# Four bias additions of a two-layer graph kernel: from GpSimd arithmetic to accumulating DMAs

## The chip, the cores and the metric

The kernel runs on one core of one Trainium2 chip. The metric is the device time of one execution in microseconds. A core has five engines with a queue of instructions each, executed in the order of the queue: TensorE (PE; its weight loads are listed as PEld), VectorE (DVE), ScalarE (ACT), GpSimd (POOL) and SyncE (SP). SP and GpSimd also issue DMAs; 16 DMA engines move the data.

## The reference, cut to what matters

There are 32 batches of 512 nodes with 256 features, in float32. Two layers follow one another, each with a graph part and a feed-forward part, and each part adds its result to x:

```python
# layer 0
x = x + gnn(layernorm(x), adj)
h = layernorm(x)
trop = piecewise(max over features of (h + Wt))          # 1024 columns
fused = g * trop + (1 - g) * gelu(h @ Wc + bc)           # g = sigmoid(h @ Wg + bg)
x = x + fused @ Wd + bd                                  # <- bd
# layer 1
h = einsum('bnd,hde->bhne', layernorm(x), W)             # 4 heads of 64
attention = softmax(leaky_relu(e_src + e_dst), masked by adj)
dst = attention @ h + bias                               # <- the bias of the values
out = relu(dst) + h
out = (out - mean) / sqrt(var + eps) * ln_gamma + ln_beta   # <- ln_beta
x = x + out
sw = softmax(layernorm(x) @ Wslice')                     # 512 columns, 64 slices of 8 heads
x = x + (sw @ scan(tokens)) @ out_w.T + out_b            # <- out_b
```

The four marked rows are the biases of this case: `bd` of layer 0's feed-forward, and of layer 1 `gnn_bias` (called abias), `ln_beta` (beta) and `out_b` (outb). As a softmax row sums to one, adding abias to the values before the weighted sum and adding it to the weighted sum afterwards give the same dst.

## The kernel before

The kernel is written in Python that is unrolled in full. A scheduling layer then orders each engine's queue with a cost model of its own and puts in the semaphores, so that the source order and the order on an engine differ; the source still steers it, by generators that are woven into one another.

**Layer 0** (`layer0_sorted`). The nodes are sorted by how many table rows they need. `feed_forwards` goes through 32 groups of 512 nodes. `sums(s, g)` gathers the group's rows into `xg` with four indirect DMAs (L553; a row has 275 numbers: 256 features, mean, count and the like). For each of four tiles of 128 nodes, ACT normalizes into `xn` (L574), GpSimd issues gathers of table rows (L564, L595), and DVE folds every row into `best` by a maximum (L598). At the end of `sums`, L609 to L610 add bd to the four tiles of `xg`, one GpSimd addition of 128 x 256 numbers each. `mixed` runs the two dense matmuls (L623), their activations (L625), and the bends of the piecewise function (L632 to L641). `down` multiplies by Wd (L652), adds the product to `xg` on DVE (L654), and stores the sum (L655). `down` of a group stands one group later than its `sums`. The convolutions of the later nodes are woven in between (L392 to L470).

**Layer 1** (`layer1_plain`). `attentions` handles one batch after another, and `prepare(b + 1)` is woven into `attention(b)`; `mixer` (the second part of the layer, `slices`, `tokens`, `scan`, `unslice`) takes two batches at a time and draws the attentions along with it: each `yield` of `mixer` names a number, which is multiplied by PACE, and so many steps of `attentions` follow.

`prepare(b)` gathers x by four indirect DMAs (L1154), normalizes it (`normed`, L1126 to L1133), and then adds beta to the stored x by one GpSimd addition of 128 x 1024 numbers (L1167). PE computes the heads' values and logits (hp, L1180) for four tiles; of each tile ACT takes three exponentials, `mine` (L1183), the factor in column HO of `hv` (L1184) and `other` (L1185), and copies the values to `ht` (L1186). Then GpSimd writes `ht` plus abias to `hv` (L1189), and DVE multiplies `hv` by the factor, in four instructions (L1202). Meanwhile `mine` goes by a PE transpose (minep, L1193), an ACT copy, a store (L1197) and four broadcasting loads (L1200) into the rows `own`, which the attention steps need.

`attention(b)` has 8 turns. In each, DVE makes two tiles of weights (`weigh`, L1213: the larger of own and other, times the mask), three turns ahead; PE multiplies them with `hv` (avp, L1249) and sums them (adp, L1254). At the end the sums are transposed back (L1232), and DVE divides into `av` (L1275). `norm(b, av)` is drawn step by step during the next batch's turns, through the list `unfinished`: its first step applies the relu and adds `ht` (L1290) and takes means (L1292 to L1294); its second gets the variance, with a power on GpSimd (L1300), and multiplies by gamma (L1301); its third scales (L1303) and adds to x (L1304). It is drawn after turns 0, 1 and 3.

`slices(b)` normalizes x again (L1126 to L1133), adds outb to the stored x with one GpSimd addition (L1328), and makes the slice weights (lgp, L1335 to L1342) and tokens (yTp, L1347). `scan` mixes the tokens (xp L1400 to vp L1557, with y at L1520 to L1522, yTp L1527, oTp L1535, msp L1543, rms L1546 and L1547). `unslice` multiplies back and adds to x (L1567, L1569), which is stored (L1570).

PSUM has two sets of four banks in layer 1: tag "pv" for attention's sums, and tag "any" for all other products (hp, x3T, x4T, lgp, minep, yTp and so on), handed out again when the last reader of a bank is done.

Of the kernel before, what the change touches and what calls it, by code (L numbers as in the profile page):

```python
# [8 lines left out]
F32 = mybir.dt.float32  # L9
# [4 lines left out]
AF = mybir.ActivationFunctionType  # L14
ALU = mybir.AluOpType
# [4 lines left out]
P = 128  # L20
N = 512
D = 256
# [75 lines left out]
def layer0_sorted(tc, ident, eps, x, adj, w, x2s, ranks, over, following):  # L98
# [29 lines left out]
    with ExitStack() as ctx:  # L128
# [4 lines left out]
        def const(name, shape, src):  # L133
            t = cst.tile(shape, F32, tag=name, name=name)
            nc.sync.dma_start(t, src)
            return t
# [3 lines left out]
        bias = const("bias", [P, D], w["bias"].partition_broadcast(P))  # L140
        bd = const("bd", [P, D], w["bd"].partition_broadcast(P))
        wc = cst.tile([P, DC, FFN], F32, tag="wc", name="wc")
# [31 lines left out]
        for c in range(CT // P):  # L174
            nc.gpsimd.affine_select(below[:, c, :], below[:, c, :], pattern=[[1, CT]], compare_op=ALU.is_gt,
                                    fill=0.0, base=-c * P, channel_multiplier=-1)

        table = dr.tile([D, FFN], F32, tag="table", name="table", bufs=1)
        least = dr.tile([2, D], F32, tag="least", name="least", bufs=1)
# [363 lines left out]
        def feed_forwards():  # L543


            def sums(s, g):
# [57 lines left out]
                for c in range(DC):  # L604
# [3 lines left out]
                                        ALU.is_gt)  # L608
                for t in range(NT):  # L609
                    nc.gpsimd.tensor_add(xg[:, t, :D], xg[:, t, :D], bd)  # L610
                got[s, g] = xg, xnT, best
# [253 lines left out]
def layer1_plain(tc, ident, eps, x2s, ranks, adj, w, out, over, ps):  # L865
# [23 lines left out]
    TURNS = AP * NT + 6  # L889
    STEPS = 15  # L890
    WANTED = 68
# [9 lines left out]
    with ExitStack() as ctx:  # L901
# [41 lines left out]
        edges = ctile("edges", [P, 2, B * NT])  # L943
        abias = const("abias", [P, AH * HO], w["gnn_bias"].rearrange("h e -> (h e)").partition_broadcast(P))
        gamma = const("gamma", [P, AH * HO], w["ln_gamma"].rearrange("h e -> (h e)").partition_broadcast(P))
        beta = const("beta", [P, AH * HO], w["ln_beta"].rearrange("h e -> (h e)").partition_broadcast(P))
        bfx = const("bfx", [P, KC, 1], w["b_fx"].rearrange("(k p o) -> p k o", p=P, o=1))
        bfx_eps = ctile("bfx_eps", [P, KC])
        nc.vector.tensor_scalar_mul(bfx_eps, bfx[:, :, 0], -1e-5)
        outb = const("outb", [P, D], w["out_b"].partition_broadcast(P))  # L950
        conv_w = const("conv_w", [P, KC, KW], w["hy_conv_w"][:DI].rearrange("(c p) k -> p c k", p=P))
# [196 lines left out]
        def prepare(b):  # L1148
# [13 lines left out]
            for i, _ in enumerate(edged):  # L1162
                if i < 3 or b not in masked:
                    yield
                if i == 2:
                    normed(xt, xn, f"c{b}")
                    nc.gpsimd.tensor_add(xt, xt, beta.unsqueeze(1).to_broadcast([P, NT, D]))  # L1167
                    yield
# [8 lines left out]
            for t in range(NT):  # L1177
                ph = psum("any", f"hp{b}_{t}")
                for c in range(DC):
                    nc.tensor.matmul(ph[:, : AH * (HO + 2)], xnT[:, c, t * P : (t + 1) * P], wa[:, c, :],  # L1180
                                     start=c == 0, stop=c == DC - 1)
                d = ph[:, AH * HO : AH * HO + AH]
                nc.scalar.activation(mine[:, :, t], ph[:, AH * (HO + 1) : AH * (HO + 2)], AF.Exp, scale=1.0 - SLOPE)  # L1183
                nc.scalar.activation(hv[:, t, :, HO], d, AF.Exp)  # L1184
                nc.scalar.activation(other[:, t, :], d, AF.Exp, scale=SLOPE - 1.0)  # L1185
                nc.scalar.copy(ht[:, t, :], ph[:, : AH * HO])  # L1186
                yield

            nc.gpsimd.tensor_add(hv[:, :, :, :HO], ht.rearrange("p t (h e) -> p t h e", h=AH),  # L1189
                                 abias.rearrange("p (h e) -> p h e", h=AH).unsqueeze(1).to_broadcast([P, NT, AH, HO]))  # L1190
            yield
            pt = psum("any", f"minep{b}")
# [6 lines left out]
            for h in range(AH):  # L1199
                nc.sync.dma_start(own[h], own_row[h].partition_broadcast(P))  # L1200
            for t in range(NT):
                nc.vector.tensor_mul(hv[:, t, :, :HO], hv[:, t, :, :HO], hv[:, t, :, HO:].to_broadcast([P, AH, HO]))  # L1202
            ready[b] = mask, ht, hv, other, own
# [12 lines left out]
        def attention(b):  # L1216
# [21 lines left out]
            for i, (q, j) in enumerate(turns):  # L1238
# [17 lines left out]
                yield  # L1256
                if unfinished and i != 2:
                    next(unfinished[0], None)
                    yield
                    if i > 2:  # L1260
                        unfinished.pop()
# [10 lines left out]
            for q in range(AP):  # L1272
                bt = back(vT[q], f"bp{q}_")
                heads = slice(2 * q, 2 * q + 2)
                nc.vector.tensor_mul(av[:, :, heads, :], bt.rearrange("p (t h e) -> p t h e", t=NT, h=2),  # L1275
                                     rs[:, :, heads].unsqueeze(3).to_broadcast([P, NT, 2, HO]))
                yield
            unfinished.append(norm(b, av))

# [38 lines left out]
        def slices(b, j, yT, rn):  # L1318
# [8 lines left out]
            xnT = yield from turned(xn, "x4T", f"x4T{b}", 1)  # L1327
            nc.gpsimd.tensor_add(xt, xt, outb.unsqueeze(1).to_broadcast([P, NT, D]))  # L1328
            sw = sb.tile([P, NT, DI], F32, tag="sw", name=f"sw{b}", bufs=1)
# [910 lines left out]
```

## Time and profile before

Each of three runs took 4456.45, 4460.33 and 4473.15 us; the median is 4460.33. The profiled execution took 4459.08 us, of which the span from the first instruction to the last is 4456.4.

| engine | busy us | share of the span |
|---|---|---|
| PE | 3922.0 | 88% |
| DVE | 3347.2 | 75% |
| ACT | 2291.6 | 51% |
| POOL | 1718.8 | 39% |

The four additions in GpSimd's table of instructions:

| line | what | count | busy us | mean ns |
|---|---|---|---|---|
| L610 | `xg` + bd, 128 x 256 | 128 | 109.6 | 861 |
| L1189 | `hv` = `ht` + abias, 128 x 1024 | 32 | 80.2 | 2506 |
| L1167 | x + beta, 128 x 1024 | 32 | 77.6 | 2424 |
| L1328 | x + outb, 128 x 1024 | 32 | 75.8 | 2370 |

A line of the timeline has the start, the time that the instructions took together, the engine, the source line, the operation, output and inputs, the shapes, the number of instructions, and in brackets the idle time of the engine before them and what ended it. A line of the list of waits has the waiting instruction, who ended the wait, and the total, the number and the longest of these waits. The chain of waits goes back from the last instruction, at each step to what released it.

### The profile page before, as it was taken

Reading aid. Unit: us, or ns where it says so; the run is one execution under the profiler, and the core shown is the slowest. Engines: PE = TensorE matmul, PEld = TensorE weight load, DVE = VectorE, ACT = ScalarE, POOL = GpSimd, SP = SyncE. Lnnn points to the kernel's source line nnn. Section 1 sums busy time; section 2 is a strip of 40 time slices with the busy share of each in tenths; the row PEclk is TensorE's granted clock in tenths of the full one; section 3 lists DMA queues with packets and bytes.
Section 4 is the critical chain, followed back from the end, with each engine's and each line's share of the span. In section 5 each row is a group of like instructions: output and inputs, shape, how many; then the busy total and the mean of one; then the engine's idle time right before and its main releaser. Section 6 shows DMA issues by size and latency. Waiting matters only on the chain.

```text
span 4456.4 us, 57911 instructions
## 1 busy us (share of the span) xinstructions
PE 3922.0 (88%) x20311; PEld 2470.6 (55%) x20311; DVE 3347.2 (75%) x7008; ACT 2291.6 (51%) x4756; POOL 1718.8 (39%) x2036
## 2 busy tenths in 40 slices
PE   5568898899988999888997899999999999999987
PEld 4454565566656656545554455555555555555555
DVE  6668887897788987877766777767677877778763
ACT  3345565566564665556654544544545444454433
POOL 2357644664446644454314232332222232332220
PEclk8679999999999999989998999999999999999998
DMA  5546543664436543564422111111111111111100
GB/s 133 160 144 223 190 130 122 210 200 139 156 117 213 187 147 129 162 201 167 138 81 67 36 53 57 56 48 58 51 43 42 53 55 55 58 48 58 41 15 16
DMA packets 235107, 474.21 MB, mean 106 GB/s; under 512 B 38299, under 2 KB 114075, under 8 KB 234804
## 3 DMA queue, kind: packets, MB, share of 16 engines
q0 software_dynamic: 98688, 315.94, 22.2%
q1 hardware_dynamic: 136116, 154.46, 11.0%
q8 instruction: 162, 2.65, 0.2%
q14 instruction: 141, 1.16, 0.1%
HBM read 413.16 MB, written 57.16 MB: 106 GB/s over the span
## 4 chain that ended last, share of the span: by engine, by line
DVE 34%; PE 32%; DMA 11%; issue 9%; POOL 9%; ACT 5%; SPq 0%; POOLq 0%; DVEq 0%; ACTq 0%
DVE att L1213 5%; DVE acc L637 4%; PE clsp L623 3%; PE avp L1249 3%; PE po L652 3%; PE gatep L623 3%; DMA rows<-table,xs 2%; PE yTp L1347 2%; DVE sw L1337 2%; DVE sw L1342 2%; DVE best L598 2%; DMA rows<-table,tops 2%; DVE sst L1340 2%; DMA best<-table,xs 2%; PE xp L1400 1%
## 5 line engine op out<-in xcount | busy, mean ns | idle before, releaser
L623 PE MATMUL clsp<-xnT,wc 128*128 128x512 f32 x1024 | 520.8, 627 | 49.7 <-ACT cls L625 37.6
L623 PE MATMUL gatep<-xnT,wg 128*128 128x512 f32 x1024 | 499.8, 607 | 10.5 <-ACT gate L625 7.7
L652 PE MATMUL po<-wd,acc 128*128 128x256 f32 x2048 | 455.4, 381 | 6.1 <-DVE acc L641 3.8
L1213 DVE SCALAR_TENSOR_TENSOR att<-own,other,mask 128x512 f32<-128x512 f32 x512 | 392.9, 796 | 79.0 <-DMA own<-ownd 79.0
L652 PEld LDWEIGHTS po<-wd,acc 128*128 128x128 f32 x2048 | 388.3, 191 | 72.1 <-issue 9.2
L598 DVE SCALAR_TENSOR_TENSOR best<-rows,xs,best 128x1024 f32<-128x1024 f32 x212 | 274.4, 1295 | 121.9 <-ACT best L592 76.4
L637 DVE SCALAR_TENSOR_TENSOR acc<-past,fld,acc 128x512 f32<-128x512 f32 x448 | 345.7, 775 | 24.9 <-ACT past L636 16.9
L632 ACT ACTIVATE acc<-tz,fld 128x512 f32<-128x512 f32 x256 | 198.8, 777 | 269.3 <-PE tz L630 240.1
L623 PEld LDWEIGHTS gatep<-xnT,wg 128*128 128x128 f32 x1024 | 196.0, 196 | 252.3 <-issue 197.9
L636 ACT ACTIVATE past<-tz,fld 128x512 f32<-128x512 f32 x448 | 291.4, 693 | 68.1 <-DVE acc L637 66.6
L1347 PE MATMUL yTp<-sw,x 128*128 128x512 f32 x512 | 264.6, 655 | 64.3 <-DVE sw L1342 59.6
L595 POOL DMA_INDIRECT rows<-table,xs x212 | 249.5, 1177 | 171.6 <-DVE best L598 119.0
L1249 PE MATMUL avp<-att,hv 128*32 128x512 f32 x2048 | 298.9, 607 | 5.6 <-DVE att L1213 5.6
L623 PEld LDWEIGHTS clsp<-xnT,wc 128*128 128x128 f32 x1024 | 181.5, 198 | 188.1 <-issue 111.8
L434 PE MATMUL pm<-h,adj 128*128 128x258 f32 (+1 forms) x1024 | 181.2, 324 | 99.9 <-DVE keep L427 33.7
L1300 POOL TENSOR_TENSOR mu<-mu,eps 128x16 f32<-128x16 f32 x32 | 111.6, 3487 | 391.1 <-DVE mu L1299 391.0
L1335 PE MATMUL lgp<-wsl,x4T 128*128 128x512 f32 x512 | 242.8, 613 | 15.7 <-ACT sw L1336 6.8
L1154 POOL DMA_INDIRECT x<-x2s,ranks x128 | 135.9, 1062 | 298.1 <-DVE att L1213 148.1
L625 ACT ACTIVATE gate<-gatep,fld 128x512 f32<-128x512 f32 x256 | 175.5, 685 | 142.6 <-PE gatep L623 123.8
L553 POOL DMA_INDIRECT xs<-rows_of,order x128 | 156.1, 1219 | 221.5 <-DVE acc L637 100.8
L1567 PE MATMUL outp<-v,swT 128*128 128x256 f32 x1024 | 227.6, 381 | 0.0
L625 ACT ACTIVATE cls<-clsp,fld 128x512 f32<-128x512 f32 x256 | 176.1, 688 | 93.9 <-PE clsp L623 55.6
(599 smaller groups left out, 8978.1 us busy)
## 6 DMA issues: line engine op xcount, KB each, us to landing
adj<-in_adj POOLq DMA_DIRECT2D x128, 256.0 KB
ai<-in_adj SPq DMA_DIRECT2D x128, 256.0 KB
own<-ownd SPq DMA_DIRECT2D x128, 256.0 KB
rows_of<-keep SPq DMA_DIRECT2D x32, 550.0 KB
x<-in_x SPq DMA_DIRECT2D x32, 512.0 KB
x2s<-xs SPq DMA_DIRECT2D x32, 512.0 KB
out<-x SPq DMA_DIRECT2D x32, 512.0 KB
rows<-table,xs POOLq DMA_INDIRECT x212
```

The lines of the kernel that those rows point to most:

```text
L595: nc.gpsimd.indirect_dma_start(out=row, out_offset=None, in_=table, in_offset=bass.IndirectOffsetOnAxis(ap=idxs[:, k : k + 1].bitcast(U32) ...
L598: nc.vector.scalar_tensor_tensor(m, row, vals[:, k : k + 1], m, ALU.add, ALU.max)
L623: nc.tensor.matmul(pf, wf[:, c, f * P : (f + 1) * P], xnT[:, c, :], start=c == 0, stop=c == DC - 1)
L625: nc.scalar.activation(o, pf, fn, bias=fld[:, f, bf : bf + 1], scale=1.0 if fn == AF.Gelu else 0.5)
L636: nc.scalar.activation(r, z, AF.Relu, bias=fld[:, f, AT + b : AT + b + 1])
L637: nc.vector.scalar_tensor_tensor(y, r, fld[:, f, CH + b : CH + b + 1], y, ALU.mult, ALU.add)
L652: nc.tensor.matmul(po[:, i, :], acc[f][:, t * P : (t + 1) * P], wd[:, f, :], start=f == 0, stop=f == FC - 1)
L1213: nc.vector.scalar_tensor_tensor(e, own[h], other[:, j, h : h + 1], mask[:, j, :], ALU.max, ALU.mult)
L1249: nc.tensor.matmul(pv[p][k * HW : (k + 1) * HW, :], hv[:, j, h, e : e + HW], weighed[b, h, j], **ends)
L1335: nc.tensor.matmul(pf, xnT[:, c, t * P : (t + 1) * P], wsl[:, c, :], start=c == 0, stop=c == DC - 1)
L1347: nc.tensor.matmul(py, xn[:, t, c * P : (c + 1) * P], sw[:, t, :], start=t == 0, stop=t == NT - 1)
L1567: nc.tensor.matmul(po[:, :D], swT[:, k, t * P : (t + 1) * P], v[:, k, :], start=k == 0, stop=k == KC - 1)
```

## The change

The rows of the four biases are put into DRAM, each repeated four times (4 KB of abias, beta or outb in one row of `added`; for bd four rows of 1 KB). An addition is then a DMA that GpSimd issues, which reads the repeated row for all 128 partitions and adds it to the tile in SBUF (`accum_op=ALU.add`): one DMA of 512 KB per group of layer 0, and three per batch of layer 1. The SBUF copies of the four rows are gone.

abias moves from the values to the weighted sum: DVE multiplies hp's values in PSUM by the factor right away, tile by tile, after ACT's exponential of that tile, which now is the first of the three; abias is added to `av` after the division, ahead of `norm`. The first step of `norm` is drawn after turn 1 instead of 0, the second after turn 2, and the third after turn 4. `prepare` has one `yield` less, and STEPS goes from 15 to 14.

```diff
-        bd = const("bd", [P, D], w["bd"].partition_broadcast(P))
...
+        bd = dr.tile([NT, D], F32, tag="bd", name="bd", bufs=1)
+        nc.sync.dma_start(bd, w["bd"].partition_broadcast(NT))
...
-                for t in range(NT):
-                    nc.gpsimd.tensor_add(xg[:, t, :D], xg[:, t, :D], bd)
+                nc.gpsimd.dma_start(xg[:, :, :D], bd.partition_broadcast(P), accum_op=ALU.add)
...
-    STEPS = 15
+    STEPS = 14
...
-        abias = const("abias", [P, AH * HO], w["gnn_bias"].rearrange("h e -> (h e)").partition_broadcast(P))
+        added = dr.tile([3, NT, D], F32, tag="added", name="added", bufs=1)
+        for i, row in enumerate((w["gnn_bias"].rearrange("h e -> (h e)"), w["ln_beta"].rearrange("h e -> (h e)"),
+                                 w["out_b"])):
+            nc.sync.dma_start(added[i], row.partition_broadcast(NT))
+        added = added.rearrange("i t d -> i (t d)")
+        ABIAS, BETA, OUTB = range(3)
+
+        def add_rows(dst, i):
+
+            nc.gpsimd.dma_start(dst, added[i].partition_broadcast(P), accum_op=ALU.add)
...
-                    nc.gpsimd.tensor_add(xt, xt, beta.unsqueeze(1).to_broadcast([P, NT, D]))
+                    add_rows(xt.rearrange("p t d -> p (t d)"), BETA)
...
+                nc.scalar.activation(hv[:, t, :, HO], d, AF.Exp)
+                nc.vector.tensor_mul(hv[:, t, :, :HO], ph[:, : AH * HO].rearrange("p (h e) -> p h e", h=AH),
+                                     hv[:, t, :, HO:].to_broadcast([P, AH, HO]))
                 nc.scalar.activation(mine[:, :, t], ph[:, AH * (HO + 1) : AH * (HO + 2)], AF.Exp, scale=1.0 - SLOPE)
-                nc.scalar.activation(hv[:, t, :, HO], d, AF.Exp)
...
-            nc.gpsimd.tensor_add(hv[:, :, :, :HO], ht.rearrange("p t (h e) -> p t h e", h=AH),
-                                 abias.rearrange("p (h e) -> p h e", h=AH).unsqueeze(1).to_broadcast([P, NT, AH, HO]))
-            yield
...
-            for t in range(NT):
-                nc.vector.tensor_mul(hv[:, t, :, :HO], hv[:, t, :, :HO], hv[:, t, :, HO:].to_broadcast([P, AH, HO]))
...
-                if unfinished and i != 2:
+                if unfinished and i not in (0, 3):
                     next(unfinished[0], None)
                     yield
-                    if i > 2:
+                    if i > 3:
                         unfinished.pop()
...
+            add_rows(av.rearrange("p t h e -> p (t h e)"), ABIAS)
             unfinished.append(norm(b, av))
...
-            nc.gpsimd.tensor_add(xt, xt, outb.unsqueeze(1).to_broadcast([P, NT, D]))
+            add_rows(xt.rearrange("p t d -> p (t d)"), OUTB)
```

More of the change, by code (lines that the diff above doesn't have):

```diff
@@ L943, in layer1_plain @@
         edges = ctile("edges", [P, 2, B * NT])
-        abias = const("abias", [P, AH * HO], w["gnn_bias"].rearrange("h e -> (h e)").partition_broadcast(P))
+        added = dr.tile([3, NT, D], F32, tag="added", name="added", bufs=1)
[6 more added lines that the diff above has]
+            nc.gpsimd.dma_start(dst, added[i].partition_broadcast(P), accum_op=ALU.add)
         gamma = const("gamma", [P, AH * HO], w["ln_gamma"].rearrange("h e -> (h e)").partition_broadcast(P))
-        beta = const("beta", [P, AH * HO], w["ln_beta"].rearrange("h e -> (h e)").partition_broadcast(P))
         bfx = const("bfx", [P, KC, 1], w["b_fx"].rearrange("(k p o) -> p k o", p=P, o=1))
@@ L949, in layer1_plain @@
         nc.vector.tensor_scalar_mul(bfx_eps, bfx[:, :, 0], -1e-5)
-        outb = const("outb", [P, D], w["out_b"].partition_broadcast(P))
         conv_w = const("conv_w", [P, KC, KW], w["hy_conv_w"][:DI].rearrange("(c p) k -> p c k", p=P))
```

## The prediction

> **What bounds the kernel now.** I read the totals by stage first. Layer 0 is mostly 300 to 2380 us, layer 1 is 2380 to 4360. Each stage gives its length, then busy time and count of PE, weight loads, VectorE (DVE), ScalarE (ACT), GpSimd (POOL), then clock, DMA share, GB/s.
>
> ```profile
> 300.00:2380.00 2080.00, 1865.12 (x7272) 1198.04 (x7270) 1680.03 (x3132) 1215.67 (x2052) 1044.08 (x1306) 0.96 0.49 159
> 2380.00:4360.00 1980.00, 1811.40 (x11810) 1077.94 (x11811) 1446.91 (x3088) 947.40 (x2440) 575.48 (x439) 0.97 0.16 50
> ```
>
> PE is busy 90% in both by this count, whose ends are modelled. Counting only columns at the spacing that full streams show (0.43 us per 512 columns, a quarter for the 32-wide tiles of L1249 and L1254) gives about 1800 us of layer 0 and 1535 of layer 1. So layer 0 is near PE's limit (1800/0.96 = 1870 of 2080), layer 1 is not (1535/0.97 = 1580 of 1980): there two in-order queues, DVE's and PE's, wait for each other. Next, who waits in layer 1 (total, times, longest):
>
> ```profile
> DVE hv L1202 <- POOL hv L1189: 177.5, 31, 9.0
> DVE att L1213 <- DMA own<-ownd: 79.0, 15, 7.3
> ```
>
> The largest wait of DVE is for the GpSimd addition of the values' bias, 5.7 us per batch. The timeline shows the two forms it takes, since batches alternate. First form:
>
> ```profile
> 3003.34 0.39 ACT L1186 COPY ht<-hp 128x256 f32<-128x256 f32 x1
> 3003.82 2.35 POOL L1189 TENSOR_TENSOR hv<-ht,abias 128x1024 f32<-128x1024 f32 x1 [2.80 <-ACT ht L1186]
> 3006.20 1.10 DVE L1202 TENSOR_TENSOR hv<-hv 128x256 f32<-128x256 f32 x3 [7.64 <-POOL hv L1189]
> ```
>
> DVE has waited since 2998.56; of that, 2.8 us lie after ACT's copy began. Second form:
>
> ```profile
> 3067.31 2.36 POOL L1189 TENSOR_TENSOR hv<-ht,abias 128x1024 f32<-128x1024 f32 x1 [2.06 <-ACT ht L1186]
> ...
> 3069.70 1.43 DVE L1202 TENSOR_TENSOR hv<-hv 128x256 f32<-128x256 f32 x4 [3.78 <-POOL hv L1189]
> 3071.99 0.16 DVE L1546 TENSOR_SCALAR rms<-msp 128x2 f32<-128x2 f32 x1 [0.86 <-PE msp L1543]
> 3078.80 0.75 DVE L1213 SCALAR_TENSOR_TENSOR att<-own,other,mask 128x512 f32<-128x512 f32 x1 [6.66 <-DMA own<-ownd]
> ```
>
> Here a second wait, for the row `own`, ends later than the first and hides it. Its source, the transpose minep (L1193), stands on PE behind 32 oTp matmuls:
>
> ```profile
> 3067.78 3.84 PE L1535 MATMUL oTp<-yT,hoT 128*128 128x128 f32 x32 [0.89 <-ACT yT L1529]
> 3071.54 0.40 PE L1543 MATMUL msp<-ms,ident 128*64 128x1 f32 x8
> 3071.87 0.28 PE L1193 MATMUL minep<-ident,mine 128*16 128x128 f32 x1
> ```
>
> Last, DVE beside a GpSimd addition: two attention steps that start with L1167's addition at 3013.33, beside minimum, median and maximum of their kind.
>
> ```profile
> 3013.50 3.52 DVE L1213 SCALAR_TENSOR_TENSOR att<-own,other,mask 128x512 f32<-128x512 f32 x2
> ```
>
> ```profile
> L1213 DVE SCALAR_TENSOR_TENSOR att<-own,other,mask x512: 652/744/2885, 2411.7 to 4296.2; 128x512 f32<-128x512 f32 x171
> ```
>
> Two cost 3.52 instead of 1.49 us: 2.0 us lost.
>
> [...] No accumulating DMA is in the trace of before.
>
> **The change part by part.** The sum is made against the profiled execution: span 4456.4, time 4459.08, 1.25 under the median 4460.33.
>
> **Values' bias.** It removes 32 GpSimd additions (80.2 us) and four multiplications per batch from SBUF (0.36 us each, L1202), and adds four from PSUM, priced by L1569 of the same size at 0.41: 128 x 0.05 = 6 us more of DVE. In the first form DVE waits for the last exponential only, about where ACT's copy begins, and has then done three of four products: 2.8 + 3 x 0.36 = 3.8 us earlier. In the second, in the build of the changed kernel minep stands right behind hp, ahead of yTp, oTp and msp: from 3071.87 to about 3067.1, `own` comes 4.7 us earlier. Over 16 pairs of batches: 16 x (3.8 + 4.7) = 136 us.
>
> **L1's beta (L1167).** 32 additions of 2.4 us go, and what DVE loses beside them: 2.0 us at 3013, 1.8 at 3106 (sw L1342, 2.48 for 0.69); 32 x 1.9 = 61 us, both places on the chain of waits. **Output bias (L1328).** 75.8 us of GpSimd; DVE instructions beside it are 7 us longer in all. The data is wanted a half batch later: nothing else. Together 136 + 61 + 7 - 6 = 198 us off DVE's queue in layer 1. What is late next is PE: with 198 less it would need 1580 of 1782 us, 89%, as full as in layer 0. I count half, 99 us: DVE and PE hold almost equal shares of layer 1's chain (762 and 729 us), so about every second microsecond won meets PE's own work.
>
> **Layer 0's bias (L610).** 128 additions (109.6 us) go. The DVE instructions that overlap one are together 47 us over the medians of their kinds. DVE holds 636 of the 2080 us of this stage's chain, so 31%: 15 us. The additions themselves hold 13 us of the chain, and the queue waits for ACT once per group, not up to four times. PE is near its limit; I take 20 of these 28.
>
> **What is added.** 32 + 96 DMA issues. On POOL one costs between 575 ns (the adjacency load L392) and 1219 (the gather L553); I take 1.0. In layer 0 each moves 512 pieces of 1 KB instead of 128 of 4 KB; between 0.6 and 4 x 0.575 = 2.3, I take 1.5. POOL does 96 + 48 instead of 343 us. Four SP loads of constants become four small ones from DRAM to DRAM: zero, they precede use by far. The landing: four gathers of 512 KB at 3088.61 had their first packet 1.7 us after the first issue, and 4 KB packets took 150 ns, eight per engine 1.2 us. Bounds: 2.9 us (as a copy) to 12 (an addition at eight times that). [...] I take 4.5.
>
> Three of the four have half a batch or more of cover. If that is gone, unslice (L1569) or layer 0's down (L654) would wait. **Only abias is short**: it is issued after DVE's product L1275, and DVE's relu step (L1290) waits for it. Between them the build has 4.8 to 5.2 us of DVE work in half of the batches and 5.6 to 8.0 in the others, at the durations of before (five to eight attention steps, two L1569), 5.9 on average; so 4.5 is covered. Ahead of it on POOL stand outb, beta or rms, whose waits end earlier in the timeline. Behind it are the batch's power (L1300) or the gathers of a later x; the gathers come 1 us later and have 12 us of DVE work before L1126 needs them. I charge 10 us for misses. The later step of norm, one fewer yield and the pace 0.887 to 0.857 only follow from this: zero, at worst a turn (126/16 = 8 us) in the tail.
>
> Sum: 4459 - 99 - 20 + 10 = 4350; with the median's 1 us, 4351. I say 4350.
>
> **The rivals.**
> **Late landing (slower).** If the accumulation takes L us, DVE idles 32 x (L - 5.9) at L1290. It eats the 109 us from L = 9.3, which is 0.95 us per 4 KB packet, over six times the gather's. At L = 11: 4350 + 163 = 4513. It would also hold up layer 0's gathers on the same engines. For it: no such row exists, and the cover is one turn. Against: DMA share is only 0.16 in layer 1.
> **Held banks.** An hp bank is now free after DVE's product, not ACT's copy; four banks serve all of hp, x4T, lgp and minep. Priced at the 1.5 us that DVE lags in the first form, 32 x 1.5 = 48: 4398. Against: DVE stands waiting at that place.
> **PE takes over (no change).** PE's own waits for DVE in layer 1 are mostly yTp for sw, 59.6 us. If a third of that is all that can be won, 4460 - 20 = 4440. Its 91% speaks for it, the streaming count against it.
> **More than half is won.** 75% of 198 and all of 28: 4460 - 148 - 28 + 10 = 4294.
>
> **How the numbers follow.** Forecast 0.45, held banks 0.15, three quarters won 0.10: faster 0.70. PE takes over: 0.13. Late landing: 0.17. What can be told from no change is 0.5%, 22 us. The range reaches from 4285 (under the best case) to 4475 (over PE's case, short of late landing).
>
> **What would show it.** L1202's successor waits under 1 us after ACT's exponential; DVE's wait for `own` falls from 79; the maximum of L1213 falls to near 750 ns; POOL's busy time falls by some 200 us; L1290 shows no wait for a DMA. I am wrong if L1290 waits 3 us or more per batch, if PE waits for banks at x4T or lgp, or if layer 0's gathers (L595) land later.

## The result, and the profile after

The changed kernel took 4498.4 us (median of 9 runs, 4485.91 to 4509.06), against 4460.33 for the kernel before: ratio 1.0085, 95% interval 1.0066 to 1.0105. It is 38 us slower where 109 us faster were forecast. The profiled execution took 4509.06 us, with a span of 4507.0.

Layer 0 is done 7.8 us earlier (last store at 2368.3 for 2376.1 us). Layer 1 loses it again: a pair of batches takes 128.6 us instead of 125.3, taken from the output stores over 13 pairs. First the two stages, with the columns of the prediction's first fence:

```profile
300.00:2380.00 2080.00, 1869.26 (x7275) 1206.88 (x7273) 1635.75 (x3141) 1216.45 (x2055) 964.82 (x1218) 0.95 0.55 168
2380.00:4360.00 1980.00, 1797.12 (x11593) 1066.87 (x11592) 1359.14 (x3032) 946.14 (x2416) 423.19 (x428) 0.96 0.29 74
```

In this window of layer 1 VectorE is busy for 88 us less (1446.91 before), GpSimd for 152 less (575.48), and the clock is 0.96 for 0.97. PE's count of instructions is lower because fewer batches fit into the window: the same work takes longer. For the same reason not all of the 88 us is work saved: over 13 whole pairs (1200.81 and 1145.85 in the windows further below) it is 55 us, or 4.2 per pair. The waits of VectorE and of PE there:

```profile
DVE sw L1344 <- ACT sw L1343: 112.2, 33, 7.0
DVE rms L1553 <- PE msp L1550: 99.8, 14, 9.9
DVE hv L1192 <- ACT hv L1191: 62.6, 54, 2.3
...
DVE av L1297 <- DMA av<-added: 28.0, 18, 5.6
...
DVE att L1218 <- DMA own<-ownd: 9.8, 10, 2.1
```

```profile
PE maskp L1092 <- DVE mask L1093: 55.6, 9, 7.1
PE lgp L1342 <- DVE mvc L1135: 21.3, 4, 6.2
PE minep L1200 <- ACT mine L1194: 19.3, 14, 2.4
```

What the change was to take away is gone: 177.5 us of waiting for GpSimd's addition have become 62.6 for ScalarE's exponential, and `own` makes 9.8 instead of 79.0. VectorE now waits elsewhere, 212 us for `sw` and `rms`, where it had waited 15 before. PE has a new kind of wait, up to 7.1 us long, for a mask copy or a statistic of VectorE (before, its largest in total, at yTp, took 3.0 us at most). The attention step has lost its slow cases (2885 ns at most before):

```profile
L1218 DVE SCALAR_TENSOR_TENSOR att<-own,other,mask x512: 655/743/800, 2401.7 to 4335.3; 128x512 f32<-128x512 f32 x171
```

One pair of batches shows how the new stall of PE comes about, in a cut of the timeline:

```profile
3476.31 0.89 POOL L953 DMA_DIRECT2D av<-added  x1 [5.49 <-DVE av L1280]
...
3481.67 1.22 DVE L1297 SCALAR_TENSOR_TENSOR av<-av,ht 128x1024 f32<-128x1024 f32 x1 [1.70 <-DMA av<-added]
...
3484.28 0.41 DVE L1576 TENSOR_TENSOR x<-x,outp 128x256 f32<-128x256 f32 x1
...
3484.71 6.80 SPq L1577 DMA_DIRECT2D out<-x  x2
...
3489.12 1.09 POOL L1162 DMA_INDIRECT x<-x2s,ranks  x1 [11.93 <-DMA out<-x]
...
3493.21 0.95 POOL L1162 DMA_INDIRECT x<-x2s,ranks  x1 [0.30 <-issue]
...
3494.17 2.95 POOL L1307 TENSOR_TENSOR mu<-mu,eps 128x16 f32<-128x16 f32 x1
...
3494.61 0.43 DVE L1134 BATCH_NORM_STATS2 stc<-x 128x6 f32<-128x256 f32 x1 [1.67 <-DMA x<-x2s,ranks]
...
3497.15 1.23 DVE L1310 TENSOR_TENSOR av<-av,mu 128x1024 f32<-128x1024 f32 x1 [0.65 <-POOL mu L1307]
...
3498.30 0.68 DVE L1093 CAST mask<-maskp 128x512 uint8<-128x512 bf16 x1
...
3499.13 2.90 PE L1342 MATMUL lgp<-wsl,x4T 128*128 128x512 f32 x3 [5.07 <-DVE mvc L1135]
```

GpSimd issues the DMA on `av` at 3476.31; VectorE's relu waits for it until 3481.67. Behind the relu on VectorE stand the outp additions, behind their fourth the store of the output, behind the store's landing four gathers of a later x, on GpSimd behind those norm's power, on VectorE behind that the scaling step, and behind that the mask copy that frees a PSUM bank. The gathers also hold VectorE up directly: it waits three times, 3.5 us in all, for rows of the later x (stc), and then only 0.65 us more for the power. PE, last in line, has been idle for 5.07 us. (The profile names mvc, which ended last before lgp; lgp does not read it. That the mask's bank is what lgp waits for is inferred: by the order of PE's products it is the next bank in turn, and the copy out of it ended at 3498.98.) And that is not all. The same stretch by windows (clock is third from the end):

```profile
3470.00:3494.50 24.50, 24.06 (x150) 17.23 (x146) 18.81 (x33) 7.23 (x18) 6.15 (x7) 1.00 0.34 93
3494.50:3498.70 4.20, 0.00 (x0) 0.00 (x0) 3.00 (x8) 1.08 (x3) 4.02 (x2) 1.00 0.35 104
3498.70:3502.10 3.40, 2.97 (x4) 1.33 (x5) 1.60 (x4) 0.00 (x0) 3.20 (x4) 0.50 0.22 55
3502.10:3510.00 7.90, 7.90 (x40) 3.14 (x41) 7.76 (x15) 5.47 (x13) 3.07 (x4) 1.00 0.57 115
```

PE does nothing for 4.2 us, and then works for 3.4 us at half the clock: three lgp matmuls of 512 columns take 2.90 us, where three in e5, an experiment below at full clock, take 1.51. The clock has two values in the traces of before and after, 1.00 and 0.50. In the 13 pairs of batches of each that are counted next, the stretches at 0.50 last 3.41, 6.83 or 10.24 us, and the idle time of PE ahead of them varies: in the kernel before, single gaps of 2.0 to 3.0 us were followed by half clock 15 times, and 11 gaps of 1.6 to 3.0 us were not.

So I count layer 1 anew. In 13 pairs of batches, from one output store to the 26th after it, the windows view gives for the kernel before, after, and two of the experiments below (with three additions by DMA, e5, and the same with norm's new turns, e10):

```profile
2583.19:4212.00 1628.81, 1512.33 (x9955) 905.93 (x9954) 1200.81 (x2575) 798.13 (x2054) 475.19 (x364) 0.98 0.16 51
```

```profile
2592.34:4263.72 1671.38, 1537.09 (x9953) 922.89 (x9951) 1145.85 (x2574) 808.11 (x2054) 364.31 (x365) 0.96 0.29 74
```

```profile
2572.72:4116.50 1543.78, 1477.43 (x9962) 895.65 (x9958) 1139.67 (x2575) 798.62 (x2054) 396.29 (x364) 1.00 0.27 72
```

```profile
2568.44:4193.71 1625.27, 1520.15 (x9958) 907.49 (x9958) 1134.93 (x2573) 800.81 (x2052) 384.91 (x361) 0.98 0.26 68
```

Taking from PE's busy time what the half-clock stretches cost (half of each; 35.8, 59.7, 0 and 39.7 us), 1476.5, 1477.4, 1477.4 and 1480.5 us are left: 113.6 to 113.9 per pair in these four. (PE is idle in part of these stretches, in 28 of after's 119.5 us, so half of each is the most that they can cost. Counting only the time in them in which PE is busy, 113.7 to 114.7 per pair are left.) Layer 1 has a floor, PE's own work, and a pair costs about this floor, plus PE's gaps, plus what the stretches at half clock cost. All kernels of this study, counted so (us per pair):

| kernel | time | ratio to before (95%) | per pair | PE's gaps | half clock | PE's own |
|---|---|---|---|---|---|---|
| before | 4460.3 | | 125.3 | 9.0 | 2.8 | 113.6 |
| after | 4498.4 | 1.0085 (1.0066 to 1.0105) | 128.6 | 10.3 | 4.6 | 113.6 |
| e1 layer 0's bias by DMA | 4442.4 | 0.9951 (0.9934 to 0.9968) | 125.8 | 9.0 | 3.2 | 113.6 |
| e2 beta and outb by DMA | 4368.9 | 0.9792 (0.9775 to 0.9809) | 118.7 | 5.0 | 0.1 | 113.6 |
| e3 values' bias by DMA | 4563.7 | 1.0226 (1.0204 to 1.0247) | 131.3 | 12.3 | 4.9 | 114.1 |
| e4 after, no abias | 4464.9 | 1.0000 (0.9988 to 1.0013) | 126.6 | 8.4 | 3.6 | 114.6 |
| e5 = e1 + e2 | 4348.8 | 0.9740 (0.9721 to 0.9759) | 118.8 | 5.1 | 0.0 | 113.7 |
| e6 = e4, old turns | 4399.9 | 0.9869 (0.9848 to 0.9889) | 122.8 | 7.0 | 2.0 | 113.8 |
| e7 = e4, old step and pace | 4452.6 | 0.9986 (0.9975 to 0.9996) | 125.8 | 7.2 | 3.8 | 114.7 |
| e8 = e4, both old | 4343.4 | 0.9735 (0.9718 to 0.9752) | 118.5 | 4.9 | 0.3 | 113.4 |
| e9 = after, both old | 4453.5 | 0.9981 (0.9971 to 0.9990) | 125.1 | 9.4 | 1.8 | 113.9 |
| e10 = e5, new turns | 4455.1 | 0.9991 (0.9977 to 1.0006) | 125.0 | 8.1 | 3.1 | 113.9 |
| e11 after, later gathers | 4487.8 | 1.0074 (1.0056 to 1.0091) | 128.7 | 11.3 | 3.8 | 113.6 |
| e12 = e5, norm earlier | 4446.4 | 0.9966 (0.9950 to 0.9981) | no trace | | | |
| e13 = e7, six x | 4496.1 | 1.0074 (1.0056 to 1.0092) | 129.3 | 10.4 | 5.9 | 113.1 |
| e14 = after, six x | 4523.2 | 1.0141 (1.0123 to 1.0160) | 130.2 | 12.0 | 5.3 | 113.0 |
| e15 = e8, six x | 4352.6 | 0.9753 (0.9733 to 0.9772) | 118.3 | 4.7 | 0.4 | 113.2 |
| e16 = e9, plain copy | 4403.8 | one run | 122.3 | 6.7 | 1.6 | 114.0 |
| e17 = after, slower pace | 4448.3 | 0.9965 (0.9955 to 0.9975) | 125.2 | 6.2 | 1.8 | 117.2 |
| e18 = e7, slower pace | 4435.9 | 0.9940 (0.9918 to 0.9963) | 124.7 | 7.7 | 2.8 | 114.3 |

The last column is a remainder and carries the errors of the modelled ends. The record of a matmul of 512 columns lasts some 600 ns, also where the next starts much earlier, so shorter waits of PE count as its work. That is the likely reason for e17's 117.2: at full clock its adp and avp start 167 and 127 ns apart on average, for 132 and 111 in e5, which makes 4.3 us per pair.

### The profile page after: what moved, and what is told of

Same layout as the page of the kernel before. It is cut to its first block, busy times and chain, and to the rows that moved or that the text cites. A ratio compares the mean times of both kernels' runs of the same rounds, so it can differ in the third digit from the quotient of the medians.

```text
span 4507.0 us, 57748 instructions
## 1 busy us (share of the span) xinstructions
PE 3947.5 (88%) x20311; PEld 2494.3 (55%) x20311; DVE 3240.3 (72%) x7008; ACT 2301.0 (51%) x4756; POOL 1491.7 (33%) x1940
## 4 chain that ended last, share of the span: by engine, by line
PE 42%; DVE 18%; DMA 12%; issue 9%; POOL 6%; ACT 5%; POOLq 0%; DVEq 0%; SPq 0%; ACTq 0%
PE clsp L623 5%; PE lgp L1342 4%; PE gatep L623 4%; PE yTp L1354 4%; PE avp L1254 4%; PE po L652 3%; DVE acc L637 3%; DMA av<-added 2%; DMA rows<-table,xs 2%; DMA best<-table,xs 2%; DVE best L599 2%; POOL x L1162 2%; PE adp L1259 2%; PE oTp L1542 1%; PE hp L1188 1%
## 5 line engine op out<-in xcount | busy, mean ns | idle before, releaser
L1218 DVE SCALAR_TENSOR_TENSOR att<-own,other,mask 128x512 f32<-128x512 f32 x512 | 359.2, 741 | 10.0 <-DMA own<-ownd 9.8
L637 DVE SCALAR_TENSOR_TENSOR acc<-past,fld,acc 128x512 f32<-128x512 f32 x448 | 332.3, 744 | 30.6 <-ACT past L636 22.4
L1342 PE MATMUL lgp<-wsl,x4T 128*128 128x512 f32 x512 | 268.2, 672 | 32.8 <-DVE mvc L1135 21.3
L1354 PE MATMUL yTp<-sw,x 128*128 128x512 f32 x512 | 232.2, 600 | 8.1 <-DVE sw L1349 6.3
L1162 POOL DMA_INDIRECT x<-x2s,ranks x128 | 147.0, 1149 | 237.8 <-DMA out<-x 122.2
L435 PEld LDWEIGHTS pm<-h,adj 128*128 128x128 f32 x1024 | 152.2, 214 | 131.2 <-issue 77.5
```

The source lines that it names most:

```text
L435: nc.tensor.matmul(pm[:, : c1 - c0], a[:, i, t * P : (t + 1) * P], h[:, i, c0:c1], start=i + c0 == 0, stop=i + 1 == NT and c0 > 0)
L637: nc.vector.scalar_tensor_tensor(y, r, fld[:, f, CH + b : CH + b + 1], y, ALU.mult, ALU.add)
L1218: nc.vector.scalar_tensor_tensor(e, own[h], other[:, j, h : h + 1], mask[:, j, :], ALU.max, ALU.mult)
L1342: nc.tensor.matmul(pf, xnT[:, c, t * P : (t + 1) * P], wsl[:, c, :], start=c == 0, stop=c == DC - 1)
L1354: nc.tensor.matmul(py, xn[:, t, c * P : (c + 1) * P], sw[:, t, :], start=t == 0, stop=t == NT - 1)
```

## The experiments

Theories after the result: **landing** (the DMA on `av` ends late, in each batch), **order** (norm's new turns, the earlier step and the pace put the in-order queues into a worse order), **contention** (accumulating DMAs disturb other transfers). Lines in an experiment's fence are those of its own kernel, a few off from after's.

### Which part loses: e1 to e4

e1 takes over only this, into the kernel before:

```diff
-                for t in range(NT):
-                    nc.gpsimd.tensor_add(xg[:, t, :D], xg[:, t, :D], bd)
+                nc.gpsimd.dma_start(xg[:, :, :D], bd.partition_broadcast(P), accum_op=ALU.add)
```

> The kernel before with layer 0's bias alone added by the accumulating DMA. The prediction's step gave it 20 us: 4440. The trace of after ended layer 0 7.8 us earlier: then 4452. If the accumulating DMAs disturb the gathers wherever they are used (the contention theory), 4460 or more.

Measured: 4442.4 us, 21 less than the 4463.4 of the kernel before in the same comparison. No disturbance; the prediction's step holds. e2, into the kernel before:

```diff
-                    nc.gpsimd.tensor_add(xt, xt, beta.unsqueeze(1).to_broadcast([P, NT, D]))
+                    add_rows(xt.rearrange("p t d -> p (t d)"), BETA)
...
-            nc.gpsimd.tensor_add(xt, xt, outb.unsqueeze(1).to_broadcast([P, NT, D]))
+            add_rows(xt.rearrange("p t d -> p (t d)"), OUTB)
```

> The kernel before with layer 1's beta and output bias alone added by DMAs; the values' bias stays on GpSimd and the steering is the old one. The prediction's steps (61 + 7 us off VectorE, half of it counted) give 4426. Both the landing theory (only the values' bias is late) and the order theory (the loss comes from the values' part and its steering) expect 4420 to 4440 here; the contention theory expects 4460 or more.

Measured: 4368.9, 94.5 us less: contention falls, and the gain is nearly three times what I had counted. Most of it shows in PE's wait at yTp for VectorE's `sw`, over 13 pairs before and then in e2:

```profile
PE yTp L1347 <- DVE sw L1342: 55.3, 31, 3.0
```

```profile
PE yTp L1356 <- DVE sw L1351: 15.2, 19, 1.0
```

`sw` is the product that took 2.48 us for 0.69 beside a GpSimd addition. PE's gaps fall by 52 us in these pairs, 40 of them here.

e3 is after with the three additions by DMA (bd, beta, outb) taken back:

```diff
-                    add_rows(xt.rearrange("p t d -> p (t d)"), BETA)
+                    nc.gpsimd.tensor_add(xt, xt, beta.unsqueeze(1).to_broadcast([P, NT, D]))
...
-            add_rows(xt.rearrange("p t d -> p (t d)"), OUTB)
+            nc.gpsimd.tensor_add(xt, xt, outb.unsqueeze(1).to_broadcast([P, NT, D]))
...
-                nc.gpsimd.dma_start(xg[:, :, :D], bd.partition_broadcast(P), accum_op=ALU.add)
+                for t in range(NT):
+                    nc.gpsimd.tensor_add(xg[:, t, :D], xg[:, t, :D], bd)
```

> The values' bias alone: product from PSUM, accumulating DMA on av, norm a turn later; the other three additions as before. Landing and order theory both put the whole loss here: 4500 to 4540, over 4460 in any case. The contention theory, with a third of layer 1's accumulating DMAs left, expects 4465 to 4480. The prediction's step (136 - 6, half of it) would give 4395.

Measured: 4563.7, 100 us more than before. The loss sits in the values' part. The parts do not simply add up, though: 100 us lost and the 115.5 won by e1 and e2 would give about 4448, and after takes 50 us more. e4 is after without the DMA on `av`:

```diff
-            add_rows(av.rearrange("p t h e -> p (t h e)"), ABIAS)
```

> After, with the values' bias left out altogether (its DMA is not issued; everything else, steering too, as in after). Landing theory: the 98 us that this DMA holds on the chain of waits go, at least half of them won: 4400 to 4450. Order theory (gathers, powers and mask copies stand badly in the queues): 4485 to 4500, no change to speak of.

Measured: 4464.9. Without its landing the kernel gains 33.5 us, outside of what order expected and short of what landing expected. The larger part, 4464.9 against the 4348 of e1 and e2 together, is neither landing nor contention.

### What in the values' part: e5 to e8, e10

e5 is e1 and e2 in one.

> The kernel before with three of the four additions by DMA (layer 0's bias, beta, output bias); the values' bias as before. If the parts add up as measured one by one (21 + 94.5 us): 4348. If they win the same time twice (PE takes over): 4365 or more. Against after without the values' bias (4465) this is then the whole price of the moved product and the new steering, some 117 us.

Measured: 4348.8; the parts add up. e6, e7 and e8 are e4 with these edits, the first, the second, and both:

```diff
-                if unfinished and i not in (0, 3):
+                if unfinished and i != 2:
...
-                    if i > 3:
+                    if i > 2:
```

```diff
-    STEPS = 14
+    STEPS = 15
...
                 yield
+            yield
             pt = psum("any", f"minep{b}")
```

> After without the values' bias, and norm drawn at the old turns (not at turn 2, finished after turn 2). If the order theory's culprit is norm's later turn, nearly all of the 117 us come back: 4350 to 4370. If it is the earlier minep and the pace, or the PSUM bank held for VectorE's product: 4450 to 4470.

> After without the values' bias, with the removed step put back ahead of minep and the pace of 15 steps; norm at the new turns. If the pace and the earlier minep are the culprit: 4350 to 4380. If norm's turn or the held bank is: 4450 to 4470.

> After without the values' bias, with both the old turns and the old step and pace: of the values' part only the product from PSUM is left. Order theory: 4340 to 4360, the level of the kernel with three DMAs, or below it. Held banks: 4430 to 4470, the loss stays.

Measured: 4399.9 (between the two expectations), 4452.6 and 4343.4. With both old, the product from PSUM costs nothing: held banks fall as a cause. Norm's turns make 109 us of the difference with the old step and pace (e7 to e8) and 65 with the new ones (e4 to e6); the step and the pace make 57 at the old turns (e6 to e8) and 12 at the new ones (e4 to e7), where the intervals of the two kernels still overlap. Together they make 121.5 us.

e8 also shows how little the wait for GpSimd's values was worth. It has neither that addition nor any abias at all, and is 5.4 us faster than e5, which has the addition and the wait; that is within the scatter of e5's runs (4338.4 to 4351.1). VectorE's waits over 13 pairs, e5 and then e8:

```profile
DVE hv L1211 <- POOL hv L1198: 144.7, 26, 7.6
DVE att L1222 <- DMA own<-ownd: 71.8, 13, 6.6
...
DVE rms L1555 <- PE msp L1552: 11.1, 13, 0.9
```

```profile
DVE att L1219 <- DMA own<-ownd: 71.8, 18, 6.9
DVE rms L1553 <- PE msp L1550: 70.2, 13, 5.7
DVE hv L1192 <- ACT hv L1191: 63.2, 49, 3.6
...
DVE sw L1344 <- ACT sw L1343: 27.1, 21, 2.2
```

The 144.7 us are gone, and 63 us for the exponential, 59 more for msp and 27 for `sw` have come: VectorE arrives earlier and waits for PE and ScalarE. PE had been working through the wait.

e10 puts the new turns, the reverse of e6's edit, into e5, and nothing else.

> The kernel with three DMAs (4349), with norm drawn at the new turns and nothing else: no product from PSUM, no landing, old step and pace. Order theory: norm's turn alone loses about what it lost without the values' bias (4453 against 4343, 109 us): 4440 to 4470. If the turn only hurts together with the product from PSUM: 4350 to 4380.

Measured: 4455.1, 106 us more than e5. Two lines of steering cost nearly all that the three DMAs won. Where, is seen at the end of outp, in e5 and then in e10:

```profile
2925.70 0.60 PE L1151 MATMUL x4T8p<-ident,x 128*128 128x128 f32 x4
...
2926.36 0.60 PE L1151 MATMUL x4T8p<-ident,x 128*128 128x128 f32 x4
...
2930.25 0.40 DVE L1578 TENSOR_TENSOR x<-x,outp 128x256 f32<-128x256 f32 x1
...
2930.80 1.95 PE L1344 MATMUL lgp<-wsl,x4T 128*128 128x512 f32 x4 [1.13 <-DVE x L1578]
...
2931.77 1.21 DVE L1299 SCALAR_TENSOR_TENSOR av<-av,ht 128x1024 f32<-128x1024 f32 x1
```

```profile
2926.27 1.22 DVE L1299 SCALAR_TENSOR_TENSOR av<-av,ht 128x1024 f32<-128x1024 f32 x1
...
2934.12 1.10 POOL L1163 DMA_INDIRECT x<-x2s,ranks  x1 [17.62 <-DMA out<-x]
...
2937.97 0.60 PE L1151 MATMUL x4T8p<-ident,x 128*128 128x128 f32 x4
...
2939.20 2.94 POOL L1309 TENSOR_TENSOR mu<-mu,eps 128x16 f32<-128x16 f32 x1
...
2942.17 1.23 DVE L1312 TENSOR_TENSOR av<-av,mu 128x1024 f32<-128x1024 f32 x1 [4.67 <-POOL mu L1309]
2943.31 0.41 DVE L1578 TENSOR_TENSOR x<-x,outp 128x256 f32<-128x256 f32 x1
...
2943.78 1.12 PE L1151 MATMUL x4T8p<-ident,x 128*128 128x128 f32 x4 [4.98 <-DVE x L1578]
```

In e5 norm's first step (L1299) follows the last of the pair's eight outp additions (L1578), and x4T runs without a gap; lgp waits 1.13 us for that addition's bank. In e10 attention is further ahead of the mixer, because `slices` draws attention on until a batch has passed norm, and this is now a turn later. Norm falls between the outp additions, its power (L1309) behind the gathers on GpSimd, the scaling step behind the power, the last outp addition behind that, and x4T, which needs that bank, 4.98 us behind on PE. Within this stall, at 2941.34, PE's clock goes to one half for 6.83 us: four x4T take 1.12 us behind it, for 0.60 ahead of it. Whether it is the source or the cost model of the scheduling layer that brings about this order was not tested.

### The price of the landing: e9 and e16

e9 is after with both edits of e8, abias added.

> The values' bias by DMA as in after, but with the old turns, the old step and the old pace: norm's first step then comes right behind av's product, with some 0.5 us of VectorE's work between them. Against 4343 without the bias: if the landing is as cheap as in after (33 us), 4376; if VectorE waits some 4.7 us of the 5.2 us landing in each batch and PE has no slack for it, 4343 + 150 = 4493. If it lies in between, about 4410, the turns were moved for a reason, and neither place is good.

Measured: 4453.5, 110 us over e8. All 32 batches wait at the relu, 82 us in all; from issue to relu it takes 5.3 us (median; 4.9 at least). The new turns do shorten the wait, to 32.1 us in after, in 19 batches, but after takes 45 us more than e9 all the same. e16 changes e9 so:

```diff
-            nc.gpsimd.dma_start(dst, added[i].partition_broadcast(P), accum_op=ALU.add)
+            nc.gpsimd.dma_start(av.rearrange("p t h e -> p (t h e)"), added[ABIAS].partition_broadcast(P))
```

> Price of adding: the kernel with the values' bias by DMA at the old turns (4454), whose DMA on av is now a plain copy of the same 512 KB (av is overwritten by the bias instead of having it added). From GpSimd's issue to VectorE's next step the adding one takes about 5.2 us. If adding costs twice the traffic at the same fixed part, 4.3 us here and some 20 us less in all; if the fixed part is nearly everything, 5.0 us or more and the same time.

(For `av` alone; beta and outb are still added. The kernel overwrites the weighted sums, so it serves for the time alone.) Measured: 4403.8 in one run, about 50 less than e9, where 20 had been expected. From issue to relu it takes 3.7 us at least, and 4.7 (median) in the batches in which the relu waits. The wait at the relu in 13 pairs is less than half of e9's, e9 first:

```profile
DVE av L1298 <- DMA av<-added: 69.7, 26, 5.2
```

```profile
DVE av L1298 <- DMA av<-added: 32.4, 25, 2.9
```

Adding costs 1.2 us per 512 KB over copying, taking the shortest of each, and 0.6 by the medians of the batches that wait. The packets point the same way: one of 4 KB took 328 ns in after's DMAs on `av`, and 159 in before's four gathers of 512 KB at 3088.61 (medians). At eight per engine that makes 1.35 us, an estimate from these two numbers.

### Why the new turns lose: e11 to e15, e17, e18

e11, on after:

```diff
             while b >= AHEAD_X and b - AHEAD_X not in stored:
                 yield True
+            if b >= AHEAD_X:
+                yield True
+                yield True
```

> After, complete, but the gathers of x that have to wait for an output's store are issued two turns later, which puts them behind norm's power in GpSimd's queue (in after ahead of it). Order theory, with GpSimd's queue as the link (store, four gathers, power, VectorE, PE, clock): the stalls of 5 to 9 us at maskp and lgp go, and a good part of the 98 us between after and after's sum of parts comes back: 4400 to 4450. If the link is another one (the phase of the two weaves itself): 4485 to 4510.

Measured: 4487.8. The power no longer waits behind the gathers, but the time hardly moves: the late gathers now delay x's statistics, ScalarE's normalization behind them, and behind that on ScalarE the `sw` that frees lgp's bank (4.04 us of PE at 2959.0). My link was one of several.

e12, on e5:

```diff
-                if unfinished and i != 2:
+                if unfinished:
...
-                    if i > 2:
+                    if i > 1:
```

> The kernel with three DMAs (4349), with norm drawn a turn earlier than before (at turns 0, 1 and 2, none left out). If a later norm only loses because it comes later, an earlier one gains: 4320 to 4345. If the old turn is a matched place, and VectorE then waits for ScalarE's squares: 4350 to 4420.

Measured: 4446.4, 98 us over e5 and outside both expectations. Earlier is as bad as later; why is open, as no profile of this one was kept. e13, e14 and e15 are e7, after and e8 with

```diff
-    AHEAD_X = 2 * GB + 1
+    AHEAD_X = 2 * GB + 2
```

and two small tiles (`sp`, `mu`) with one buffer instead of two, for the space.

> After without the values' bias, with norm at the new turns and the old step and pace (4453), and a sixth buffer for x, so that the gathers of a later batch no longer wait for the store of an output. Theory of the store (new turns bring the gathers ahead of the store's end; they hold GpSimd's queue, behind them the power, behind it VectorE, then PE): 4345 to 4380. Theory of the phase (the two weaves are out of step whatever the gathers do): 4430 to 4460.

> After, complete, with a sixth buffer for x. Theory of the store: about 100 us come back, 4390 to 4430; what is left against 4343 is then the landing and the earlier minep. Theory of the phase: 4480 to 4510.

> Control: after without the values' bias at the old turns, step and pace (4343), with the sixth buffer. Theory of the store: nothing waits for a store there, so 4335 to 4350. If the sixth buffer brings something of its own, below 4335; if it puts the queues in another, worse order, above 4360.

Measured: 4496.1, 4523.2 and 4352.6. As a test of the store these are void: in e13's trace the gathers of a batch one further on stand at the same place, and still start 4.5 us after an output store's issue (3095.45 after 3090.99; in after a store took 3.63 us), with the power behind them at 3100.35. They show that the arrangement of the slow kernels gets worse by it and that of e8 does not. The last two change one number of after and of e7:

```diff
-    PACE = 1.04 * GB * (TURNS + STEPS) / WANTED
+    PACE = 0.96 * GB * (TURNS + STEPS) / WANTED
```

> After, complete, all four additions by DMA, with one number changed: the pace at which attention is drawn, 0.96 for 1.04 of what it needs. In the build seven of the eight outp additions then stand ahead of norm on VectorE's queue, as in the kernels of 4343 to 4352, not two of them. Theory of the phase: PE's stalls at maskp and lgp and most of the half clock go; with 33 us for the landing 4375 to 4420. If it is norm's later turn as such that costs, wherever the outp additions stand: 4480 or more.

> After without the values' bias, new turns, old step (4453), with the same pace of 0.96. Theory of the phase: 4340 to 4365, the level of the old turns, although norm is drawn at the new ones. If the later turn as such costs: 4430 to 4460.

Measured: 4448.3 and 4435.9, 50 and 17 us less than after and e7. e17 lies between the two expectations, e18 where the turn as such puts it; the phase alone is not the cause. In e18 the outp additions are ahead of norm again and the stall at x4T is gone (3.6 us per pair in e7, 0 here), but another of 4.6 us per pair stands at lgp:

```profile
2704.89 1.92 POOL L31 TENSOR_TENSOR rsc<-rsc,eps 128x4 f32<-128x4 f32 x1
2706.84 0.16 DVE L1139 SCALAR_TENSOR_TENSOR shiftc<-mvc,rsc 128x4 f32<-128x4 f32 x1 [0.95 <-POOL rsc L31]
...
2707.04 0.60 ACT L1141 ACTIVATE hv<-x,shiftc,rsc 128x256 f32<-128x256 f32 x1 [21.04 <-DVE shiftc L1139]
...
2707.54 0.56 ACT L1151 COPY x4T<-x4T4p 128x512 f32<-128x512 f32 x1
...
2708.16 2.07 PE L1342 MATMUL lgp<-wsl,x4T 128*128 128x512 f32 x2 [4.84 <-DVE mu L1299]
```

ScalarE has waited 21.04 us at the normalization of the next x for its statistics, and x4T's copy, which lgp needs, stands behind it in the queue. PE stalls for 4.84 us.

What this leaves: in each slow kernel looked at, norm or the gathers of a later x bring a step that is not ready to the front of an in-order queue (GpSimd's in after and e10, ScalarE's in e11 and e18), ahead of something that PE needs; only the queue and the place differ. Without the DMA on `av`, the old turns at the old pace show no such stall: PE's longest gap is 1.7 us in e5 and 2.5 us in e8. That this chain explains every one of the slow kernels is argued from single stretches; for e12 nothing is known. That no retuning could rid the new turns of it is not shown.

## Why the prediction was wrong, point by point

The step that failed is the price of the steering: norm's later turns, one fewer yield and the pace, put at zero, make 121.5 us. With the landing, 23.5 us dearer than charged, they account for nearly all of the 147 us between the forecast (109 us faster) and the result (38 slower). The rest of the sum came out right by luck: the DMAs and the product without steering and landing were to win 119 us, and win 117 (e8), because two errors of 60 us cancel, the values' bias (5 for 65) and beta with outb (94.5 for 34).

**"Layer 1 is not near PE's limit".** This was wrong. I counted columns at the spacing of full streams and got 1535 us in 1980. The sum itself is wrong: the spacing as I stated it, 0.43 us per 512 columns and a quarter of that for the 32-wide tiles, applied to every matmul of that window, gives about 1720 us (for layer 0 it gives about the 1800 that I had). Even with vp and uTp taken at their own closer spacing (113 ns for 256 columns, 56 for 128) it is about 1640. Which columns I left out is not known. On top of it come the spacings of short matmuls: in e5 the 64 adp of a pair start 132 ns apart on average, where this spacing gives 107, and the 32 dtp of 8 columns 40 ns, where it gives 7. What PE's records leave as its own work is 113.6 us per pair (113.0 to 114.7 in all kernels but e17), some 1795 us of that window, so the busy column, 1811, which I set aside as modelled, was the better number. Of 125.3 us per pair, 11.7 could be won, 187 us in all, and only where a change shortens PE's gaps.

**Values' bias, 136 - 6 us, half counted.** 5.4 us (e5 to e8), not clear of the scatter. The wait was real and is gone, but PE was working through it; in the prediction's words, PE takes over, for this part.

**Beta and outb, 68 us, half counted.** 94.5 us (e2). VectorE's busy time fell by 4.7 us per pair, close to the 4.25 that 68 us make. But these came where PE stood waiting, most of them at yTp: its gaps fell by 4.0 us per pair and half clock by another 2.6, together 6.6 of 6.6. The rival "PE takes over" had named that wait, 59.6 us, and set its worth too low: almost three quarters of it went, not a third, and the clock gave more. "Half of it meets PE's own work" was wrong in both directions: which wait ends at PE decides, not a share.

**Layer 0, 20 us.** 21 us (e1): right.

**Norm's later step, one fewer yield and the pace, "zero, at worst a turn in the tail": the step that failed.** 109 us for the turns and 12 for the rest, on the way from e8 to e4 (by way of e6, 57 for the step and the pace and 65 for the turns). This is the term that turned the sign. I took these edits as following from the rest, priced them by their own instructions, which are the same, and did not ask what the shift of one weave against the other does to the order of each queue.

**The landing, 10 us for misses.** 33.5 us (e4 to after). I took 4.5 us, an estimate of mine between bounds of 2.9 and 12, and it is 5.2; the cover was about as short as I had worked out, and 19 of 32 batches wait. Late landing, as a rival, named the side, but its mechanism was to decide from 9.3 us on. It was also not only VectorE's wait that it cost: in the cut above the relu holds the outp addition and the store behind it.

In sum: -94.5 - 21 (e5: 4348.8), -5.4 for the product and the addition left out (e8: 4343.4), +109.2 for the turns (e7), +12.3 for step and pace (e4), +33.5 for the landing: 4498.4.

Of the signs I had named, `own`, the attention step's maximum (800 ns) and GpSimd's busy time (1491.7 from 1718.8) came as forecast. VectorE's product waits for ScalarE's exponential a little over 1 us on average (62.6 us in 54 waits), where I had said under 1. The relu, which was to show no wait for a DMA, waits 1 us per batch on average, under the 3 that I had set as the mark. One that was to prove me wrong, PE waiting for banks at lgp, is the one that came.

**The best version** is e5: three of the four additions by DMA, the values' bias and all steering as before. It takes 4348.8 us, 0.974 of the kernel before (0.972 to 0.976). (e8 and e15 leave abias out.)

## What to carry to other kernels

When an engine's busy share is 90% in a stage, take its own work as a floor and ask of each wait whether that engine is idle at its end; a long wait of another engine that it covers is worth next to nothing (5 us of 136), and a short one that it does not cover is worth more than its length. Treat an edit that only shifts one instruction stream against another as a change of its own and try it alone: here two lines of it undid three good edits. And the DMA in place of arithmetic paid here where the data is wanted much later (beta, outb, layer 0), and not between two steps of one chain.

## What was not expected of the hardware

- The half clock comes after short gaps. In the kernel before, gaps of 2.0 to 3.0 us, and a pair of gaps of 0.96 and 1.61 us, were followed by 3.41 or 6.83 us at half clock; in after, gaps of 5 to 9 us by up to 10.24. In after it is on for 119.5 us of 13 pairs, with PE busy in 91 of them. It takes 3.5 to 4.6 us per pair beside 10.3 of gaps: a microsecond of PE's gaps cost 1.3 to 1.5 there.
- An accumulating DMA of 512 KB into SBUF (128 pieces of 4 KB) let the waiting relu start 5.2 us (median in after) after its issue began, 4.9 at least in e9, a plain one 3.7 us at least (e16). The issue on `av` took GpSimd 0.84 to 1.0 us, that of the plain copy 0.56 to 0.62, and that of 512 pieces of 1 KB in layer 0 about 1.4.
- 96 such DMAs in layer 1 raised the DMA share from 0.16 to 0.29. The 64 of e2 raised it to 0.27 and did no harm that its time shows.
